# A graph kernel whose edges are sorted further ahead of their scatter, with x loaded after the scatters

## The chip, the cores and the metric

The kernel runs on one core of one Trainium2 chip. The metric is the device time of one execution in microseconds (us), the median of several runs. A core has five engines with an instruction stream each: PE multiplies matrices, DVE and ACT do elementwise work, POOL issues the scatters here, and SP issues most of the loads. Each engine runs its own instructions in order, and waits for the others by semaphores.

## The reference

6,250 nodes have 128 features each (x), and 206,250 edges have 128 features each. The edge features are summed onto the node that the edge starts from, and a small network is applied to each node. Cut to what matters:

```python
edge_aggr = jnp.zeros((n, HIDDEN)).at[src].add(edge_attr_128)
combined = jnp.concatenate([x, edge_aggr, global_expand], axis=-1) @ W_c + b_c
h = jax.nn.softplus(combined @ W1 + b1)
h = jax.nn.softplus(h @ W2 + b2)
return layernorm(x + (h @ W3 + b3))
```

The source nodes come in no useful order, and nothing is known of them before the launch, so the kernel has to sort the edges on the chip.

## The kernel before, in words

**Sorting.** The edges lie as 1,692 columns of 122 edges, and two columns are a *pair*: 846 pairs in 282 *pieces* of up to three pairs. Each pair goes through five steps. `load_rows` loads 8 pairs of edge rows from `in_edge` into a row buffer (`rows`, of which there are `ROWS` = 4), issued on SP. `code_rows` writes each row's code beside it (ACT, L1068). `compare` makes a one-hot matrix `sort_hot` from the positions of the edges (half on DVE at L1094, half on ACT at L1101 and L1103). `gather` multiplies it with the rows on PE (L1114), which puts the rows in the order of their buckets, into one of three PSUM banks. `settle` copies them on ACT (L1126) into one of `SETS` = 6 places, `pairs`. `scatter_row` then writes them with an indirect DMA from POOL (L1143) into `rows_by`, a table in DRAM with a stretch for every *bucket* of 196 nodes. A place is free again once its scatter has landed.

**Summing.** When a visit's scatters are done, `load(j)` reads up to eight chunks of 128 rows back from `rows_by` into one of six `chunks` buffers (SP). `match` compares their codes with the nodes (DVE, `hot`, L942), `product` multiplies on PE (`part`, L965), and `add` adds the result into `sums_t` (DVE, L988). A `part` matmul in the program is two instructions in the trace.

**The nodes.** After the last scatter come thirteen tiles of up to 512 nodes: `z_of(1, ...)` multiplies `x_t` (x turned, 128 x 6250) and `sums_t` with weights on PE (L1306 and L1307), two more layers follow (L1310, L1345), then x is added from `x_sb`, and the rows are normalised and stored. The sums of the last visits are done between these tiles. POOL adds the last bias to `x_sb` ahead of that.

**What sets the order.** On PE, DVE, ACT and SP the order of the instructions is written out by a plan, since each engine keeps to it. The plan gives each pair a scatter time, 1.3 us apart from 24 us on, and puts each step in at a fixed time ahead of that:

```python
SCATTER = 1.3
LOADED, CODED, COMPARED, GATHERED, SETTLED = 36.0, 21.0, 17.5, 14.0, 10.5
```

`when(t, step)` collects the steps, and they are sorted by time. The times only make the order; what an instruction waits for is set by its data. Chunk loads follow their last scatter's planned time by 11 us, matches and products come 9 and 10.5 us later. Every load on SP is issued by `sync_dma` (L283). `weights` loads the weights and x_t at planned time 100.

**Names that the text uses.** `first_at` is the planned scatter time of each load of rows, `begins` that of each piece. `pair_sets[i % SETS]` is the place of piece i. `node_rows_of` loads x for a tile of nodes (L293, its issue at L296). `ahead` is the pool that holds what the node tiles need, and `STRIDE` the number of chunks of 128 rows from one bucket's stretch in `rows_by` to the next bucket's.

Of the kernel before, what the change touches and what calls it, by code (L numbers as in the profile page):

```python
# [7 lines left out]
F32 = mybir.dt.float32  # L8
# [10 lines left out]
P = 128  # L19
# [32 lines left out]

FILL, DUE = 3, 8
ROW = 136
SETS = 6
FILL_BUCKETS = 4
FILLS, SLACK = 30.0, 60.0
HALF = 4
# [1 line left out]

SCATTER = 1.3
LOADED, CODED, COMPARED, GATHERED, SETTLED = 36.0, 21.0, 17.5, 14.0, 10.5
FIRST = 24.0
SOON, FLAGGED = 4.0, 15.9
SHARE = 2
# [9 lines left out]

SUMS = 2

ROWS = 4
BANKS = 3

TABLES = 6
# [61 lines left out]
def kernel(  # L143
# [115 lines left out]
    w_sb = {n: of_weights[n] for n in ("w1", "w2", "w3")}  # L259
    cols = of_weights["cols"]  # L260

    x_t = const.tile([P, N], F32, name="x_t")
    fold = const.tile([P, 2, D], F32, name="fold")
    z_bias = const.tile([P, 1], F32, name="z_bias")
    neg_z = const.tile([P, 1], F32, name="neg_z")
# [23 lines left out]
    def in_blocks(of, n0, lo, hi, r):  # L289
        at = next(k for k, (a, _) in enumerate(blocks) if a == n0 + lo * P) - lo  # L290
        return of[:r, at + lo:at + hi, :]

    def node_rows_of(pool, n0, n, bufs, load=sync_dma):  # L293
        t = pool.tile([P, 4, D], F32, name="x_sb", bufs=bufs)
        for lo, hi, r in blocks_of(n):
            load(t[:r, lo:hi, :], in_blocks(x, n0, lo, hi, r))  # L296
        return t

    sums_p = ctx.enter_context(tc.tile_pool(name="chunks", bufs=AHEAD))
    hots = ctx.enter_context(tc.tile_pool(name="hots", bufs=6))  # L300
# [8 lines left out]
    with ExitStack() as phase:  # L309
# [556 lines left out]
        def sum_steps():  # L866
# [36 lines left out]
            def load(j):  # L903
                v, col, _, all_of = loads[j]
                t = sums_p.tile([P, LOAD_CHUNKS, ROW], F32, name="chunks")
                chunks[j] = t
                assert len(scattered) >= col // 2
                at, q = [], 0
                while q < len(all_of):
                    of, b, c = all_of[q]  # L910
                    n = sum((o > 0) == (of > 0) and (of > 0 or x == b) for o, x, _ in all_of)
                    at.append((q, n, first_chunk(b + 1, True) + 2 * c if of else first_chunk(b) + c))
                    q += n
                for a, n, r in at:
                    ins = sync_dma(t[:, a:a + n].rearrange("p j c -> p (j c)"),
                                   rows_by[r * P:(r + n) * P, :].rearrange("(p j) c -> p (j c)", p=P))
                    late = scattered[max(0, col // 2 - LANES):col // 2] if col // 2 > awaits[0] else []
                    awaits[0] = max(awaits[0], col // 2)
                    for one in late:
                        tc.add_manual_dep(ins, one.name, SYNC, reason="every row is there")  # L920
                    apart(ins, "direct", ["scatter"], late)
# [233 lines left out]
        with tc.manual_schedule(engines={ET.PE, ET.DVE, ET.Activation, ET.SP}):  # L1155
# [31 lines left out]
            for i, (_, _, k) in enumerate(pieces):  # L1187
# [3 lines left out]
                    now += SCATTER  # L1191
                ends.append(now)
            first_at = [t for t, i, j in at_time][::LOAD_COLS // 2]
            early = [i for i, t in enumerate(first_at) if t < LOADED]
            last_pair = len(pieces) - 1
            load_rows(early[0])
# [3 lines left out]

            def weights():
                sync_dma(weights_sb, weights_in)
                for a in range(0, N, TURNED):
                    b = min(N, a + TURNED)
                    sync_dma(x_t[:, a:b], x_turned[:, a:b])

            assert G > 6
            events = []
# [5 lines left out]
                for k, step in enumerate(steps):  # L1214
                    when(t0 + (k + 0.5) / len(steps) * (t1 - t0), step)

            for i, t in enumerate(first_at):
                if t >= LOADED:
                    when(t - LOADED, lambda i=i: load_rows(i))
                when(t - CODED, lambda i=i: code_rows(i))  # L1220
            for i, t in enumerate(begins):
                mine = units(i)
                for u, unit in enumerate(mine):
                    late_by = SCATTER * pieces[i][2] * u / len(mine)
                    soon = 0.0 if i or u else SOON
                    when(t - COMPARED + late_by - soon, lambda unit=unit: compare(unit))
                    when(t - GATHERED + late_by - 1.7 * soon, lambda unit=unit: gather(unit))
                    when(t - SETTLED + late_by, lambda unit=unit: settle(unit))
# [67 lines left out]
    def node_layers(sums, ready):  # L1296
# [6 lines left out]
        def z_of(layer, n0, w):  # L1303
            z = bank()
            if layer == 1:
                nc.tensor.matmul(z[:, :w], fold[:, 0, :], x_t[:, n0:n0 + w], start=True, stop=False)  # L1306
                nc.tensor.matmul(z[:, :w], fold[:, 1, :], sums_t[:, n0:n0 + w],  # L1307
                                 start=False, stop=True)
            else:
                nc.tensor.matmul(z[:, :w], w_sb["w2"], h1.pop(n0)[:, :w], start=True, stop=True)  # L1310
            sub_z[layer, n0] = [z]
# [82 lines left out]
        with tc.manual_schedule(engines={ET.PE, ET.DVE, ET.Activation, ET.SP}):  # L1394
            part_of = {t: k for k, part in enumerate(parts) for t in part}
            now, steps = None, list(sums)

            def summed_to(k, most=None):
                while steps and ready() < sum(tiles[k]) and most != 0:
                    steps.pop(0)()  # L1400
                    most = most and most - 1

            for n0, w in tiles:
                x_of[n0] = node_rows_of(ahead, n0, w, len(tiles), load=nc.scalar.dma_start)
                for lo, hi, r in blocks_of(w):
                    nc.gpsimd.tensor_tensor(
                        x_of[n0][:r, lo:hi, :], x_of[n0][:r, lo:hi, :],
                        b3_all[:r].unsqueeze(1).to_broadcast([r, hi - lo, D]), op=ALU.add)
            summed_to(0)
            z_of(1, *tiles[0])  # L1410
            normed = None
            for step in range(len(tiles) + 2):
                first, second, third = (tiles[k] if 0 <= k < len(tiles) else None
                                        for k in (step, step - 1, step - 2))
                if step + 1 < len(tiles):
                    summed_to(step + 1, FIRST_STEPS)
                if second:
                    z_of(2, *second)
                if third:
                    k = part_of[third]  # L1420
                    if third == parts[k][0]:
                        now = open_part(parts[k])
                    last_product(*third)
                for layer, tile_ in ((1, first), (2, second)):
                    if tile_:
                        decay(layer, *tile_)
                        log1p(layer, *tile_)
                if third:
                    last_layer(now, *third)
                    if third == parts[k][-1]:  # L1430
                        normed = (now, k >= len(parts) - 2, k == len(parts) - 1)
                if step + 1 < len(tiles):
                    summed_to(step + 1)
                    z_of(1, *tiles[step + 1])
                for layer, tile_ in ((1, first), (2, second)):
                    if tile_:
                        softplus(layer, *tile_)
                if normed:
                    norm(*normed)
                    normed = None  # L1440
# [123 lines left out]
```

## Time and profile before

| | |
|---|---|
| median of 3 runs | 1329.86 us (1329.32 to 1330.11) |
| profiled execution, its own time | 1331.48 us |
| its span in the trace | 1329.7 us |
| mean granted TensorE clock | 0.953 |
| scatters (L1143) | 846, 978 ns each |
| moved by DMA | 386.29 MB, mean 291 GB/s |
| chunk loads issued on SP | 735 |

The profile is of one execution. A busy time is the sum of an engine's instructions; the rest of the span is idle time, which costs only where the engine is the one that the others wait for. A chain of waits is followed back from the last instruction: at each step to what released it.

### The profile page before, as it was taken

Reading aid. Unit: us, or ns where it says so; the run is one execution under the profiler, and the core shown is the slowest. Engines: PE = TensorE matmul, PEld = TensorE weight load, DVE = VectorE, ACT = ScalarE, POOL = GpSimd, SP = SyncE. Lnnn points to the kernel's source line nnn. Section 1 sums busy time; section 2 is a strip of 40 time slices with the busy share of each in tenths; the row PEclk is TensorE's granted clock in tenths of the full one; section 3 lists DMA queues with packets and bytes.
Section 4 is the critical chain, followed back from the end, with each engine's and each line's share of the span. In section 5 each row is a group of like instructions: output and inputs, shape, how many; then the busy total and the mean of one; then the engine's idle time right before and its main releaser. Section 6 shows DMA issues by size and latency. Waiting matters only on the chain.

```text
span 1329.7 us, 27151 instructions
## 1 busy us (share of the span) xinstructions
PE 1190.0 (89%) x8677; PEld 1127.4 (85%) x8677; DVE 1080.9 (81%) x2418; ACT 1067.6 (80%) x2484; POOL 880.4 (66%) x915
## 2 busy tenths in 40 slices
PE   5886888878999889988899999999989999999893
PEld 4776887877999889988799999989989999998762
DVE  7867988998899979798788887889857657787774
ACT  5896999899987899876999989979889999403354
POOL 2776777777776677765777777767767777820334
PEclk9768999989999899998999999999989999999996
DMA  8899999999999999999999999999999999975421
GB/s 215 255 278 352 317 314 306 314 281 353 337 310 306 342 348 351 334 322 281 327 281 298 327 311 327 324 296 327 330 317 294 314 336 318 341 213 148 137 86 52
DMA packets 226901, 386.29 MB, mean 291 GB/s; under 512 B 29660, under 2 KB 138916, under 8 KB 226368
## 3 DMA queue, kind: packets, MB, share of 16 engines
q1 hardware_dynamic: 183009, 264.95, 66.2%
q0 software_dynamic: 41328, 115.65, 24.8%
q10 hardware_dynamic: 2415, 3.87, 0.9%
q8 instruction: 73, 1.20, 0.4%
q14 instruction: 76, 0.62, 0.1%
HBM read 239.37 MB, written 149.57 MB: 292 GB/s over the span
## 4 chain that ended last, share of the span: by engine, by line
PE 41%; DMA 28%; DVE 16%; ACT 7%; issue 5%; POOL 3%; SPq 1%; ACTq 0%; DVEq 0%; POOLq 0%
PE part L965 24%; DMA chunks<-rows_by 12%; PE sorted L1114 12%; DMA rows<-in_edge 10%; DMA rows_by<-pairs,pair 5%; ACT pairs L1126 4%; DVE hot L942 3%; POOL rows_by L1143 3%; ACT sort_hot L1101 2%; DVE sort_hot L1094 1%; DVE pair_ib L486 1%; DVE past L715 1%; DVE sums_t L988 1%; PE small L545 1%; PE small L547 1%
## 5 line engine op out<-in xcount | busy, mean ns | idle before, releaser
L1143 POOL DMA_INDIRECT rows_by<-pairs,pair x846 | 827.8, 978 | 326.2 <-issue 202.3
L965 PE MATMUL part<-hot,chunks 128*128 128x196 f32 x3576 | 683.5, 335 | 9.9 <-DVE sums_t L988 7.0
L1126 ACT COPY pairs<-sorted 64x387 f32<-64x387 f32 (+2 forms) x1144 | 544.2, 476 | 81.9 <-PE sorted L1114 62.5
L965 PEld LDWEIGHTS part<-hot,chunks 128*128 128x128 f32 x3576 | 591.2, 192 | 18.9 <-DVE sums_t L988 8.4
L1114 PE MATMUL sorted<-rows,sort_hot 122*128 122x129 f32 x3384 | 506.7, 290 | 52.5 <-ACT pairs L1126 43.4
L1114 PEld LDWEIGHTS sorted<-rows,sort_hot 122*128 122x128 f32 x3384 | 461.1, 200 | 65.2 <-ACT pairs L1126 62.6
L942 DVE TENSOR_TENSOR hot<-chunks,both_ps 128x784 f32<-128x784 f32 (+3 forms) x558 | 436.3, 803 | 20.6 <-DMA chunks<-rows_by 20.2
L1101 ACT ACTIVATE sort_hot<-plain,slot 122x128 f32<-122x128 f32 x846 | 279.0, 393 | 11.4 <-DMA rows<-in_edge 5.5
L988 DVE TENSOR_TENSOR sums_t<-sums_t,part 128x392 f32<-128x392 f32 (+1 forms) x262 | 144.0, 549 | 130.6 <-PE part L965 129.2
L1103 ACT ACTIVATE sort_hot<-sort_hot,ones 122x384 f32<-122x384 f32 (+2 forms) x286 | 175.1, 612 | 9.3
L1094 DVE TENSOR_TENSOR sort_hot<-slot,both_ps 122x384 f32<-122x384 f32 (+2 forms) x286 | 155.0, 543 | 3.8 <-PE sorted L1114 3.2
L486 DVE TENSOR_TENSOR pair_ib<-pair_block,both_ps 122x512 bf16<-122x512 bf16 (+2 forms) x157 | 103.9, 667 | 0.3
L1387 POOL TENSOR_SCALAR y<-y,mv,rs 128x128 f32<-128x128 f32 x40 | 31.3, 789 | 108.2 <-issue 79.0
L564 DVE TENSOR_REDUCE slot<-small 122x16 f32<-122x512 f32 (+2 forms) x109 | 73.1, 671 | 15.0 <-PE small L547 14.8
L1317 ACT ACTIVATE away<-sorted,z_bias 128x512 f32<-128x512 f32 (+2 forms) x13 | 8.5, 656 | 77.7 <-PE sorted L1307 77.7
L545 PE MATMUL small<-pair_ib,half 122*122 122x512 bf16 (+2 forms) x109 | 44.2, 405 | 15.8 <-DVE slot L564 15.6
L1068 ACT COPY rows<-pair_i 122x16 f32<-122x16 f32 x106 | 22.7, 215 | 30.5 <-DMA rows<-in_edge 29.5
L547 PEld LDWEIGHTS <-starts_h 128*122 128x122 bf16 x236 | 26.0, 152 | 17.8 <-issue 13.5
L715 DVE TENSOR_TENSOR past<-both_ps,starts 128x512 f16<-128x512 f32 (+1 forms) x61 | 40.1, 668 | 0.8 <-PE small L730 0.6
L730 PEld LDWEIGHTS <-past 128*128 128x128 f16 x424 | 25.5, 100 | 17.0 <-DVE past L715 11.8
L730 PE MATMUL small<-jump,past 128*128 128x56 f16 (+3 forms) x424 | 29.4, 191 | 10.7 <-DVE past L715 7.8
L715 DVE TENSOR_TENSOR past<-both_ps,starts_late 128x512 f16<-128x512 f32 (+2 forms) x49 | 32.5, 665 | 0.0
(162 smaller groups left out, 522.5 us busy)
## 6 DMA issues: line engine op xcount, KB each, us to landing
rows<-in_edge SPq DMA_DIRECT2D x105, 903.0 KB
chunks<-rows_by SPq DMA_DIRECT2D x431, 136.0 KB
chunks<-rows_by SPq DMA_DIRECT2D x229, 204.0 KB
rows_by<-fill SPq DMA_DIRECT2D x21, 816.0 KB
chunks<-rows_by SPq DMA_DIRECT2D x52, 272.0 KB
rows_by<-pairs,pair POOLq DMA_INDIRECT x846
rows<-in_edge SPq DMA_DIRECT2D x105, 80.6 KB
rows_by<-fill SPq DMA_DIRECT2D x14, 544.0 KB
```

The costliest lines, as they stand in the source:

```text
L486: nc.vector.tensor_tensor(ib, pair_block[:, cols].unsqueeze(2).to_broadcast([PN, n, SB]), iota_ps[:PN, :SB].unsqueeze(1).to_broadcast([PN, ...
L564: nc.vector.tensor_reduce(to, of, axis=mybir.AxisListType.X, op=ALU.max)
L715: nc.vector.tensor_tensor(past[:, :, a:b], twice_ps[:KB].unsqueeze(1).unsqueeze(1).to_broadcast([KB, 2, b - a, P // 2]), own["starts"][:, ...
L942: nc.vector.tensor_tensor(hot[:, q - a:q - a + m], chunks[j][:, lo:hi + 1:step, D:W].to_broadcast([P, m, BL]), iota_ps.unsqueeze(1).to_bro ...
L965: nc.tensor.matmul(part[:, b - base_of[v], :], t[:, place_in(j, q), :D], hot[:, q - a], start=first, stop=last)
L988: nc.vector.tensor_add(here, here, of)
L1094: nc.vector.tensor_tensor(hot[:PN, :m], slot[:PN, at:at + 2 * m - 1:2].unsqueeze(2).to_broadcast([PN, m, P]), slot_ps[:PN].unsqueeze(1).to ...
L1101: nc.scalar.activation(hot[:PN, j], by_slot[:PN], AF.Abs, bias=slot[:PN, at:at + 1], scale=-1.0)
L1103: nc.scalar.activation(hot[:PN, :m], hot[:PN, :m], AF.Relu, bias=ones[:PN, :1], scale=-1.0)
L1114: nc.tensor.matmul(out[:, j, :], hot[:PN, j], rows_at[col // LOAD_COLS][:PN, col % LOAD_COLS, :], start=True, stop=True)
L1126: nc.scalar.copy(sets_at[i][64 * n:64 * n + 64, lo:lo + m, h, :W], out[64 * h:64 * h + 64, :m, :])
L1143: s = nc.gpsimd.indirect_dma_start(out=dst, out_offset=bass.IndirectOffsetOnAxis(ap=at, axis=0), in_=rows[:, j].rearrange("p a b -> p (a b ...
```

## The change

It does four things.

1. A function `earlier(t)` is taken off the planned times of `load_rows`, `code_rows`, `compare`, `gather` and `settle`. It is 0 up to a planned time of 44 us, grows by a tenth of the time from there, and stays at 14 us, or eleven pairs, from 184 us on. Scatters, chunk loads, matches and products keep their planned times.
2. There are eleven places for settled rows and five row buffers. Room comes from `x_t`, which held 25,000 bytes of each partition from the start and is now allocated in `ahead`.
3. x_t is no longer loaded by `weights` on SP. After the last settle, ACT issues x_t (three transfers of 1,024 KB and one of 53 KB) and all of x in one tile `x_rows` (three of 1,024 KB and one of 64 KB), in the place of 15 transfers into `x_sb`. POOL's addition of the bias follows on slices of `x_rows`.
4. Two chunk loads of the same shape whose rows lie `STRIDE` apart, those of two neighbouring buckets, are issued as one transfer with one more dimension.

```diff
-SETS = 6
+SETS = 11
+EARLIER, EASE, EASED = 14.0, 0.1, 20.0
-ROWS = 4
+ROWS = 5
...
-    x_t = const.tile([P, N], F32, name="x_t")
...
-                for a, n, r in at:
-                    ins = sync_dma(t[:, a:a + n].rearrange("p j c -> p (j c)"),
-                                   rows_by[r * P:(r + n) * P, :].rearrange("(p j) c -> p (j c)", p=P))
+                while at:
+                    a, n, r = at.pop(0)
+                    if at and at[0][1:] == (n, r + STRIDE):
+                        at.pop(0)
+                        b, r = divmod(r, STRIDE)
+                        ins = sync_dma(
+                            t[:, a:a + 2 * n].rearrange("p (h j) c -> p h (j c)", h=2),
+                            rows_by.rearrange("(s r) c -> s r c", r=STRIDE * P)[
+                                b:b + 2, r * P:(r + n) * P, :].rearrange("s (p j) c -> p s (j c)", p=P))
+                    else:
+                        ins = sync_dma(t[:, a:a + n].rearrange("p j c -> p (j c)"),
+                                       rows_by[r * P:(r + n) * P, :].rearrange("(p j) c -> p (j c)", p=P))
...
+            def earlier(t):
+                return max(0.0, min(EARLIER, EASE * (t - FIRST - EASED)))
...
             def weights():
                 sync_dma(weights_sb, weights_in)
-                for a in range(0, N, TURNED):
-                    b = min(N, a + TURNED)
-                    sync_dma(x_t[:, a:b], x_turned[:, a:b])
...
-            for i, t in enumerate(first_at):
-                if t >= LOADED:
+            for i, at in enumerate(first_at):
+                t = at - earlier(at)
+                if at >= LOADED:
                     when(t - LOADED, lambda i=i: load_rows(i))
                 when(t - CODED, lambda i=i: code_rows(i))
-            for i, t in enumerate(begins):
+            for i, at in enumerate(begins):
+                t = at - earlier(at)
                 mine = units(i)
...
+            x_t = ahead.tile([P, N], F32, name="x_t")
+            x_rows = ahead.tile([P, len(blocks), D], F32, name="x_rows")
+            for a in range(0, N, TURNED):
+                b = min(N, a + TURNED)
+                nc.scalar.dma_start(x_t[:, a:b], x_turned[:, a:b])
+            for a in range(0, len(blocks), TURNED // P):
+                b = min(len(blocks), a + TURNED // P)
+                nc.scalar.dma_start(x_rows[:, a:b, :], x[:, a:b, :])
+            x_of["t"] = x_t
...
-                x_of[n0] = node_rows_of(ahead, n0, w, len(tiles), load=nc.scalar.dma_start)
+                k = by_block.index(n0)
+                x_of[n0] = x_rows[:, k:k + -(-w // P), :]
```

Three places show how the order moves. The first is SP's queue around the load of the weights. Here `rows<-in_edge` is a load of edge rows (two instructions for one), `chunks<-rows_by` a chunk load, and `rows_by<-fill` clears rows of the table. Before:

```order
L283 DMA chunks<-rows_by 128x136 x12
L283 DMA rows_by<-fill 128x4x408
L283 DMA weights_sb<-in_weights 128x900
L283 DMA x_t<-in_x_turned 128x2048 x3
L283 DMA x_t<-in_x_turned 128x106
L283 DMA rows<-in_edge 112x4x516
L283 DMA rows<-in_edge 10x4x516
L283 DMA chunks<-rows_by 128x136 x4
```

After:

```order
L283 DMA chunks<-rows_by 128x2x136 x6
L283 DMA rows<-in_edge 112x4x516
L283 DMA rows<-in_edge 10x4x516
L283 DMA rows_by<-fill 128x4x408
L283 DMA weights_sb<-in_weights 128x900
L283 DMA rows<-in_edge 112x4x516
L283 DMA rows<-in_edge 10x4x516
L283 DMA chunks<-rows_by 128x2x136 x2
```

The four pieces of x_t are gone, a load of rows stands ahead of the weights that stood behind them, and twelve and four chunk loads are six and two of twice the size. In the whole program SP's chunk loads go from 735 to 689.

The second is PE's queue at the end of the sorting. `sorted<-rows,sort_hot` is a gather (L1114 before, L1117 after), `part<-hot,chunks` a product of the sums (L965 before, L968 after), and `small<-most_of,ones` a count at the end. Before:

```order
L1114 MATMUL sorted<-rows,sort_hot 128x129 x3
L965 MATMUL part<-hot,chunks 128x196 x4
L1114 MATMUL sorted<-rows,sort_hot 128x129 x4
L965 MATMUL part<-hot,chunks 128x196 x24
L1241 MATMUL small<-most_of,ones 1x48
L965 MATMUL part<-hot,chunks 128x196 x128
L1306 MATMUL sorted<-x_t,fold 128x512
```

After:

```order
L1117 MATMUL sorted<-rows,sort_hot 128x129 x3
L968 MATMUL part<-hot,chunks 128x196 x4
L1117 MATMUL sorted<-rows,sort_hot 128x129 x4
L968 MATMUL part<-hot,chunks 128x196 x49
L1247 MATMUL small<-most_of,ones 1x48
L968 MATMUL part<-hot,chunks 128x196 x128
L1312 MATMUL sorted<-x_t,fold 128x512
```

Behind the last gather stand 49 products where 24 stood, ahead of the same count; from there on the order is the same.

The third is ACT's queue at its last settles (`pairs<-sorted`, with the number of the place) and the loads of x. Before:

```order
L1126 COPY pairs_111<-sorted 64x2x129 x4
L296 DMA x_sb<-in_x 128x512 x11
L296 DMA x_sb<-in_x 128x128
L296 DMA x_sb<-in_x 120x128
L296 DMA x_sb<-in_x 128x256
L296 DMA x_sb<-in_x 114x128
```

After:

```order
L1129 COPY pairs_117<-sorted 64x2x129 x4
L1413 DMA x_t<-in_x_turned 128x2048 x3
L1413 DMA x_t<-in_x_turned 128x106
L1416 DMA x_rows<-in_x 128x2048 x3
L1416 DMA x_rows<-in_x 128x128
```

x_t now comes from this queue, ahead of x itself, in 8 issues for the 15 before, with 6.4 MB for 3.2.

More of the change, by code (lines that the diff above doesn't have):

```diff
@@ L291, in in_blocks @@
         return of[:r, at + lo:at + hi, :]
[L293 to L297, printed above, removed]
     sums_p = ctx.enter_context(tc.tile_pool(name="chunks", bufs=AHEAD))
@@ L1305, in z_of @@
             if layer == 1:
-                nc.tensor.matmul(z[:, :w], fold[:, 0, :], x_t[:, n0:n0 + w], start=True, stop=False)
+                nc.tensor.matmul(z[:, :w], fold[:, 0, :], x_of["t"][:, n0:n0 + w], start=True, stop=False)
                 nc.tensor.matmul(z[:, :w], fold[:, 1, :], sums_t[:, n0:n0 + w],
@@ L1401, in summed_to @@
                     most = most and most - 1
+            x_t = ahead.tile([P, N], F32, name="x_t")
[7 more added lines that the diff above has]
+            x_of["t"] = x_t
+            by_block = [n0 for n0, _ in blocks]
             for n0, w in tiles:
-                x_of[n0] = node_rows_of(ahead, n0, w, len(tiles), load=nc.scalar.dma_start)
+                k = by_block.index(n0)
+                x_of[n0] = x_rows[:, k:k + -(-w // P), :]
                 for lo, hi, r in blocks_of(w):
```

## The prediction

> **What bounds the kernel now.** I read the page's busy shares first, then the busy time by stretches, the chain of waits, the waits of each engine, and last the issues on SP and ACT around the places that the diff touches. The profiled execution took 1331.48 us, 1.62 us above the median of the three timed runs (1329.86); its span is 1329.7 us, so 1.8 us lie outside the span, and I leave them as they are.
>
> From the page, the busy time of the engine that works longest:
>
> ```profile
> PE 1190.0 (89%) x8677; PEld 1127.4 (85%) x8677; DVE 1080.9 (81%) x2418; ACT 1067.6 (80%) x2484; POOL 880.4 (66%) x915
> ```
>
> PE has 1329.7 - 1190.0 = 139.7 us in which it does no matmul. Nothing in the diff takes matmuls away, so a gain has to come out of these 139.7 us (or out of a better clock). The busy time by stretches says where they lie; the first column is the stretch and its length, then PE, PEld, DVE, ACT, POOL, the granted clock, the busy share of the DMA engines and GB/s:
>
> ```profile
> 50.00:650.00 600.00, 522.09 (x4125) 494.93 (x4126) 523.80 (x1273) 522.96 (x1234) 429.60 (x439) 0.93 0.99 318
> 650.00:1150.00 500.00, 486.83 (x3525) 478.63 (x3524) 382.80 (x687) 456.57 (x1076) 374.23 (x384) 0.98 1.02 315
> 1150.00:1330.00 180.00, 149.84 (x788) 127.29 (x786) 135.63 (x311) 55.30 (x95) 55.94 (x69) 0.94 0.47 144
> ```
>
> Three stages with three limits. Before 650 us PE is idle for 600 - 522.09 = 77.9 us; there the DMA engines are busy 0.99 of the time, and DVE and ACT are as busy as PE. From 650 to 1150 us PE is idle for 13.2 us in 500: this stage is PE's. After 1150 us it is idle for 30.2 us. So what saves time in the first stage lets PE arrive earlier at its full stretch, and what only lets the scatters run ahead of PE late in the kernel saves nothing. The waits say the same for POOL, which issues the scatters (engine and line, what it waited for, us in total, times, longest):
>
> ```profile
> POOL rows_by L1143 <- issue: 202.3, 661, 1.2
> DVE sums_t L988 <- PE part L965: 129.2, 112, 8.2
> POOL rows_by L1143 <- ACT pairs L1126: 56.4, 44, 7.2
> PE sorted L1114 <- ACT pairs L1126: 43.4, 39, 2.5
> ```
>
> 661 of the 846 scatters wait for nothing but their own issue, and 56.4 us is all that POOL ever waited for sorted rows to be settled. That is the most that settling them earlier can give POOL, and only a part of it reaches the end, since 112 times DVE waited for PE's sums.
>
> **The change part by part.**
>
> *x_t leaves the early SP queue.* The SP queue around its load, then the chain of waits there and later, each with start and length, and the POOL wait that followed:
>
> ```profile
> 101.38 3.88 SPq L283 DMA_DIRECT2D x_t<-in_x_turned  x4
> 105.38 1.64 SPq L283 DMA_DIRECT2D rows<-in_edge  x2
> 108.49 6.73 SPq L283 DMA_DIRECT2D chunks<-rows_by  x4
> ```
>
> ```profile
> 108.88 16.11 DMA chunks<-rows_by
> 125.08 0.56 DVE hot L942
> ...
> 132.55 6.72 DMA rows<-in_edge
> ...
> 140.17 4.18 DMA chunks<-rows_by
> ...
> 542.98 13.53 DMA rows<-in_edge
> 556.52 11.29 DMA chunks<-rows_by
> ...
> 588.08 15.07 DMA chunks<-rows_by
> ```
>
> ```profile
> 134.29 0.97 POOL L1143 DMA_INDIRECT rows_by<-pairs,pair  x1 [7.00 <-ACT pairs L1126]
> ```
>
> The four pieces of x_t (3.2 MB) stand ahead of a rows load and of the chunk loads, and the first chunk load behind them takes 16.11 us, on the chain; thirty us later one takes 4.18. POOL then stands for 7.00 us, its longest wait for settled rows. I price the stall by PE's idle time:
>
> ```profile
> 100.00:150.00 50.00, 34.84 (x306) 31.04 (x302) 41.92 (x119) 39.31 (x93) 32.96 (x35) 0.90 1.02 340
> 150.00:300.00 150.00, 128.61 (x1073) 121.11 (x1074) 134.99 (x327) 139.06 (x328) 114.37 (x118) 0.97 0.96 305
> ```
>
> In the 50 us of the load PE is idle for 15.16 us, and in the next 150 us for 21.39, or 7.13 in 50. The load costs 15.16 - 7.13 = **8.0 us**, which go. The ends: 3.9 us, if only SP's own issue time goes, and 16.11 - 4.18 = 11.9 us.
>
> *Sorting up to 14 us earlier, eleven places, a fifth row buffer.* Loads, codes, comparisons, gathers and settles move ahead together, so the distances between them stay; what grows is the lead over the scatter. It eases in from 44 us on, and what is pulled ahead of the chunk work then is work that PE does anyway. The price shows at PE's end: 49 part matmuls stand behind the last sort where 24 stood. Each is two instructions in the trace. The chain of waits there:
>
> ```profile
> 1144.32 0.99 PE sorted L1114 x8
> 1145.31 7.96 PE part L965 x48
> 1153.27 0.17 PE small L1241 x2
> 1153.45 10.49 PE part L965 x62
> ...
> 1164.29 3.13 DMA chunks<-rows_by
> ...
> 1171.28 27.13 PE part L965 x162
> 1198.41 0.86 PE sorted L1306 x2
> ```
>
> One instruction takes 7.96 / 48 = 0.166 us, so 25 x 2 x 0.166 = 8.3 us of work moves behind the last sort. It is not new work: PE reaches the last sort that much earlier if it was busy up to there, and the 30.2 us that PE idles at the end have room for it. I take 0, with +8.3 as the end at which those 8.3 us are not got back. What the lead can take away is a stall that feeds itself: a late chunk holds DVE, PE and with them the next sort, the scatters come late, and so do the chunks that wait for them. Settled rows in hand for 11 pairs more let POOL go on. Between 300 and 650 us,
>
> ```profile
> 300.00:650.00 350.00, 317.90 (x2466) 306.19 (x2466) 308.67 (x722) 299.28 (x706) 245.54 (x251) 0.96 1.01 328
> ```
>
> PE idles for 32.1 us; that and 0 are the ends. But the DMA engines are busy 1.01 of the time there, so a lead cannot make the bytes come faster. The one excess that a row buffer and a lead cover plainly is the rows load of 13.53 us at 543 us, against the 6.72 us of the one at 132.55: **6.8 us**, which I take; the chunk loads of 11.29 and 15.07 us behind it wait for scatters and stay. The fifth buffer also eases SP, by its own waits:
>
> ```profile
> SPq L283 <- PE part L965: 228.2, 118, 8.4
> SPq L283 <- PE sorted L1114: 158.0, 41, 16.6
> ```
>
> The 158.0 us are waits for a row buffer that PE still reads, and chunk loads and fills are queued behind them. I count them inside the 6.8, because SP also waits for 228.2 us on PE's parts and so would stand later.
>
> *Two alike chunk loads in one.* SP's chunk issues fall from 735 to 689. At 6.73 / 4 to 0.39 us each, the 46 that go are 18 us or more of SP's time, but SP stands 386 us in the two waits above. I take 0, with -2 and +1 as ends, the latter for a tile whose first half must now wait for its second. Bytes and packets stay.
>
> *x_t and x behind the scatters.* ACT now issues 8 transfers with 6.4 MB after its last settle, where it issued 15 with 3.2 MB:
>
> ```profile
> 1146.76 15.91 ACTq L296 DMA_DIRECT2D x_sb<-in_x  x12
> ```
>
> ACT has nothing else to do then. The stage in which they land:
>
> ```profile
> 1150.00:1200.00 50.00, 48.22 (x283) 46.34 (x282) 44.34 (x69) 0.00 (x0) 19.44 (x20) 1.00 0.80 246
> ```
>
> At 246 GB/s for a share of 0.80, a full share is 307 GB/s, so the added 3.2 MB are 10.4 us of DMA time, and 0.20 x 50 = 10 us were free. PE does not touch x_t before 1198.41, fifty us after the issue. The cover for the chunk loads is their six buffers: 8 chunks of two instructions each are 2.7 us a buffer, 13 us for five. A chunk load of 3.13 us stands on the chain already, so I take **+1**; the ends are 0 and +10.4, if the transfers push the chunk loads back by all that they take.
>
> Here a rule speaks against the change. The Trainium skill, DMA: Bandwidth & Descriptors, section Issuing engines are not separate DMA queues, says that transfers from all issuing engines run on the same 16 DMA engines, and that another issuer saves only the time it takes to issue. The row above with 3.88 us on SP is that issue time; by the rule x_t would save 3.9 us early and give back 10.4 late, +6.5 instead of -7. That the early stall of 16.11 us stands on the chain and the tail has a free fifth is why I do not take it.
>
> **The sum.** -8.0 - 6.8 + 0 + 0 + 1.0 = -13.8 us. 1331.48 - 13.8 = 1317.7 for an execution like the profiled one, and 1.62 less against the median: **1316 us**. The forecast's own range has x_t at its two ends and the lead between 0 and half of the 32.1 us: -3.9 + 0 + 1 = -2.9 gives 1327, -11.9 - 16 + 1 = -26.9 gives 1303.
>
> **The rivals.**
>
> *The stall breaks altogether (faster).* If the lead and the buffers remove all 32.1 us from 300 to 650 us as well as the 8.0 before, the sum is -40.1 and the time 1290 us. For it: the chain from 543 to 603 us is DMA and scatters, link after link, which is what a self-feeding stall looks like. Against it: the DMA share of 1.01.
>
> *The bytes are only moved (slower).* The mechanism is the queue of transfers at 1146 us: 6.4 MB from ACT beside the last chunk loads. It decides once a chunk load lands more than 13 us after it was free to go, the cover above. Then PE, at its full stretch there (48.22 of 50 us), starves for up to the 10.4 us, the 25 parts behind the last sort are work on the path (+8.3), and from the early stage only 3.9 us come back: +14.8 in all, 1344.7 us, or 1336.4 without the parts. I set it at 1341. For it: one chunk load on the chain in this stage already, and a DMA share of about 1 in all stages ahead, so that a stall removed early may simply return. Against: the free fifth. The Trainium skill's rule on issuing engines leads here.
>
> *Nothing changes.* If the DMA engines set the pace from 50 to 1150 us (0.99 and 1.02), the sorting lead is refilled at the same rate, and x_t's DMA time comes back in the tail: the time stays at 1330, give or take 2.7 us. Against it: GB/s differ between stretches of like share (305 to 340), so the share is no hard limit.
>
> **How the numbers follow.** Forecast 0.50, stall broken altogether 0.15, nothing changes 0.08, slower 0.27. A measurement of this kernel tells 0.2%, some 2.7 us, from no change. The forecast and the first rival are faster: 0.65; the same 0.08; slower 0.27. The range takes the forecast, most of the way to the first rival, and the slower rival up to its 1341: 1297 to 1341. It leaves out about 0.10 below and 0.09 above.
>
> **What would show it.** Right: no chunk load near 16 us on the chain around 109 us, POOL's 7.00 us wait gone, PE's idle time from 100 to 150 us near 7 us, and the last sort on PE about 20 us earlier than 1144 us (13.8 of gain, 8.3 of parts). POOL's waits for settled rows well under 56.4 us, without the end moving by as much. The first L1306 follows the parts without waiting for x_t. Wrong: PE busy under 45 us in the 50 us behind the last sort, with chunk loads of over 13 us on the chain there; or the last sort where it was, with the DMA share still at 1; or SP's wait for PE's sorts still near 158 us.

## The result: slower by 0.7%, and the profile after

| | before | after |
|---|---|---|
| median of 7 runs each | 1330.2 us (1329.32 to 1331.99) | 1341.06 us (1338.01 to 1347.99) |
| ratio, 95% interval | | 1.0073 (1.0046 to 1.0101) |
| profiled execution, its span | 1331.48, 1329.7 us | 1343.9, 1342.1 us |

The forecast was 1316 us. The time is that of the rival named slower, 1341, but not by its mechanism alone; that the number agrees is in part luck.

The page of the kernel after, and its busy time by stretches (columns as in the prediction):

```profile
PE 1194.4 (89%) x8677; PEld 1131.4 (84%) x8677; DVE 1080.6 (81%) x2418; ACT 1065.2 (79%) x2489; POOL 877.3 (65%) x915
```

```profile
50.00:650.00 600.00, 519.49 (x4087) 492.48 (x4086) 515.84 (x1256) 525.19 (x1244) 431.45 (x443) 0.93 0.97 312
650.00:1150.00 500.00, 486.53 (x3517) 478.56 (x3516) 383.28 (x691) 451.37 (x1066) 371.36 (x382) 0.98 1.01 311
1150.00:1342.00 192.00, 157.82 (x831) 134.25 (x829) 141.87 (x319) 55.19 (x95) 53.73 (x66) 0.94 0.50 161
```

PE's idle time in the first two stages has not moved: 80.5 us for 77.9 and 13.5 for 13.2. The last stage is longer, with more work in it and more idle time (34.2 us for 30.2). The chain of waits of the kernel after says where:

```profile
1143.22 0.89 PE sorted L1117 x8
1144.11 3.00 PE part L968 x18
1147.13 11.30 DMA chunks<-rows_by
...
1159.35 8.99 DMA chunks<-rows_by
...
1168.36 7.34 DMA chunks<-rows_by
...
1178.25 4.15 DMA chunks<-rows_by
...
1184.06 27.13 PE part L968 x162
1211.19 0.86 PE sorted L1312 x2
```

Before, the last sort ended at 1145.31 us and the first node tile began at 1198.41: 53.1 us. After, they are at 1144.11 and 1211.19: 67.1 us. From there to the end of the span it is 131.3 us before and 130.9 after. So the 12.4 us between the two spans are made in the stretch between the last sort and the first node tile: it is 14.0 us longer, while the last sort ends 1.2 us earlier and the end is 0.4 shorter. By the medians the kernel is only 10.9 us slower. With the same stretch and end, the last sort of a typical execution then comes some 2.7 us earlier (14.0 - 0.4 - 10.9, an estimate); the forecast had said about 20. Of the 14.0, 50 instructions of 0.166 us are 8.3: the 25 products that moved. The other 5.7 are waits, and four chunk loads of 4 to 11 us stand on the chain where one of 3.13 stood.

The early load of x_t did go. The first row is the wait that POOL had at 134.29 us, the second the stretch from 100 to 150 us:

```profile
133.73 0.97 POOL L1146 DMA_INDIRECT rows_by<-pairs,pair  x1 [0.30 <-issue]
```

```profile
100.00:150.00 50.00, 37.13 (x338) 33.21 (x337) 42.99 (x120) 45.45 (x109) 38.10 (x40) 0.97 0.87 284
```

POOL goes on after its own 0.30 us there. But PE is idle for 12.87 us in this stretch, not for 7. The products that the order had here stand later: PE works on products for 8.59 us in it, and for 13.47 in the run *x alone* below, which has x_t late and no lead. Long chunk loads are not gone either: the chain followed back from 140 us has one of 14.60 us, from 121.61 on.

The waits of the kernel after:

```profile
PE sorted L1117 <- ACT pairs L1129: 59.2, 55, 2.7
...
POOL rows_by L1146 <- ACT pairs L1129: 55.5, 49, 7.0
```

POOL waited for settled rows for 55.5 us where it waited for 56.4. A lead of eleven pairs in the plan has not become a lead on the chip. It can be measured pair by pair, from the end of the last settle of a pair's piece to the start of its scatter: on the mean of the 846 pairs this is 2.67 us before and 2.44 after (2.81 in a second profile of the kernel after), and never more than 7.1. PE's wait for ACT's settles has grown from 43.4 to 59.2 us. ACT's instructions near the end of the sorting, and POOL's scatters of the first piece in them, suggest why (start, length, what, how many in a row):

```profile
1127.96 1.97 ACT L1129 COPY pairs<-sorted 64x387 f32<-64x387 f32 x4
1129.95 0.99 ACT L1104 ACTIVATE sort_hot<-plain,slot 122x128 f32<-122x128 f32 x3
1130.97 0.62 ACT L1106 ACTIVATE sort_hot<-sort_hot,ones 122x384 f32<-122x384 f32 x1
1131.49 0.20 ACT L1071 COPY rows<-pair_i 122x12 f32<-122x12 f32 x1
1131.70 1.96 ACT L1129 COPY pairs<-sorted 64x387 f32<-64x387 f32 x4
1133.68 0.99 ACT L1104 ACTIVATE sort_hot<-plain,slot 122x128 f32<-122x128 f32 x3
1134.70 0.62 ACT L1106 ACTIVATE sort_hot<-sort_hot,ones 122x384 f32<-122x384 f32 x1
1135.33 1.96 ACT L1129 COPY pairs<-sorted 64x387 f32<-64x387 f32 x4
```

```profile
1130.85 0.97 POOL L1146 DMA_INDIRECT rows_by<-pairs,pair  x1 [0.30 <-issue]
1132.12 0.97 POOL L1146 DMA_INDIRECT rows_by<-pairs,pair  x1 [0.30 <-issue]
```

The first piece is settled at 1129.93, and its first scatter starts 0.92 us later. Nothing is free on ACT in these rows: a piece of three pairs takes it 1135.33 - 1131.70 = 3.63 us, and 3.74 where it also writes codes. POOL's cadence of 0.97 + 0.30 us makes 3.81 for the same three scatters. ACT gains 0.07 to 0.18 us a piece on POOL, so by this estimate a lead of 14 us takes 78 to 200 pieces without a stall (the trace has 286 pieces, of four settles each), and a single stall can take it away. ACT is not alone in this. From 650 to 1150 us it is busy for 451.37 of 500 us and PE for 486.53, and in the chain of the kernel before PE takes 1.33 + 0.67 us for half a piece and its share of products, 4.0 for a piece.

SP's waits:

```profile
SPq L283 <- PE part L968: 290.6, 130, 8.5
...
SPq L283 <- PE sorted L1117: 78.3, 32, 13.8
SPq L283 <- DVE hot L945: 55.5, 11, 13.8
```

SP's waits for PE's sorts fell by 79.7 us, which is the fifth buffer's doing (with four they are 175.4 in the run *after, four row buffers*). Its waits for PE's parts grew by 62.4 us, and those for DVE's `hot` by 35.9 (19.6 before).

### The profile page after: what moved, and what is told of

Read it like the earlier page. It is cut to its first block, busy times and chain, and to the rows that moved or that the text cites. A ratio compares the mean times of both kernels' runs of the same rounds, so it can differ in the third digit from the quotient of the medians.

```text
span 1342.1 us, 27057 instructions
## 1 busy us (share of the span) xinstructions
PE 1194.4 (89%) x8677; PEld 1131.4 (84%) x8677; DVE 1080.6 (81%) x2418; ACT 1065.2 (79%) x2489; POOL 877.3 (65%) x915
## 4 chain that ended last, share of the span: by engine, by line
PE 37%; DMA 24%; DVE 12%; POOL 9%; issue 8%; ACT 8%; SPq 1%; ACTq 0%; POOLq 0%; DVEq 0%
PE part L968 21%; PE sorted L1117 11%; DMA rows_by<-pairs,pair 10%; POOL rows_by L1146 9%; DMA chunks<-rows_by 9%; ACT pairs L1129 5%; DMA rows<-in_edge 3%; DVE hot L945 2%; ACT sort_hot L1104 2%; DMA rows_by<-fill 2%; DVE sort_hot L1097 1%; DVE slot L558 1%; PE small L539 1%; DVE past L709 1%; DVE pair_ib L480 1%
## 5 line engine op out<-in xcount | busy, mean ns | idle before, releaser
L968 PE MATMUL part<-hot,chunks 128*128 128x196 f32 x3576 | 689.6, 337 | 14.2 <-DVE sums_t L991 11.0
L968 PEld LDWEIGHTS part<-hot,chunks 128*128 128x128 f32 x3576 | 597.3, 194 | 23.5 <-DVE sums_t L991 13.0
L1117 PE MATMUL sorted<-rows,sort_hot 122*128 122x129 f32 x3384 | 506.7, 290 | 63.7 <-ACT pairs L1129 59.2
L1117 PEld LDWEIGHTS sorted<-rows,sort_hot 122*128 122x128 f32 x3384 | 460.7, 201 | 79.2 <-ACT pairs L1129 78.4
```

What stands on the lines that cost most here:

```text
L968: nc.tensor.matmul(part[:, b - base_of[v], :], t[:, place_in(j, q), :D], hot[:, q - a], start=first, stop=last)
L1117: nc.tensor.matmul(out[:, j, :], hot[:PN, j], rows_at[col // LOAD_COLS][:PN, col % LOAD_COLS, :], start=True, stop=True)
```

## The experiments

Two theories. *Late parts*: the lead never comes about, and the 25 products that it puts behind the last sort are work on the path. *x in the tail*: the 6.4 MB beside the last chunk loads are the loss. Single executions differ in when the last sort is done (1144.1 and 1138.6 us in two profiles of the kernel after, on two chips); the stretch from the last sort to the first node tile repeats to within a microsecond there (67.1 and 66.7 us), so it is read from the profiles and the times from the medians. Each ratio is to the kernel before on the same chip. In the table, the runs marked A were made on one chip and those marked B on another; for the first two rows the chip is not known.

| run | chip | products between last sort and first node tile | that stretch, us | ratio to before, 95% interval |
|---|---|---|---|---|
| before | | 152 | 53.1 | |
| after | | 177 | 67.1 | 1.0073 (1.0046 to 1.0101) |
| after, again | B | 177 | 66.7 | 1.0106 (1.0064 to 1.0148) |
| x alone | A | 152 | 56.5 | 1.0000 (0.9970 to 1.0030) |
| merged loads alone | A | 152 | 53.1 | 0.9998 (0.9968 to 1.0027) |
| x, fifth row buffer | B | 152 | 61.8 | 1.0037 (1.0008 to 1.0066) |
| after without the lead | A | 152 | 61.2 | 1.0036 (1.0010 to 1.0062) |
| the same, four row buffers | A | 152 | 57.1 | 0.9998 (0.9973 to 1.0024) |
| after, four row buffers | B | 177 | 65.0 | 1.0097 (1.0062 to 1.0131) |
| after, half the lead | A | 164 | 63.4 | 1.0060 (1.0034 to 1.0087) |
| after without x | A | 177 | 59.2 | 1.0048 (1.0020 to 1.0076) |
| after, x in three lots | A | 177 | 60.5 | 1.0086 (1.0053 to 1.0120) |

**x alone.** Places, row buffers, lead and chunk loads are as before; the edit is to the kernel after, with cuts marked.

```diff
-SETS = 11
+SETS = 6
...
-EARLIER, EASE, EASED = 14.0, 0.1, 20.0
+EARLIER, EASE, EASED = 0.0, 0.1, 20.0
...
-ROWS = 5
+ROWS = 4
...
-                    if at and at[0][1:] == (n, r + STRIDE):
+                    if False:
```

> The kernel before with x_t and x loaded from ACT after the last settle, and nothing else of the change. Theory (late parts): the loss is the 25 products behind the last sort, since the lead over the scatters never comes about; x alone then gains 8 us early and loses some 5 in the tail: 1325 to 1330 us. Rival (x in the tail): the 6.4 MB beside the last chunk loads are the loss and the early gain is given back by the shared transfers: 1337 to 1343 us, with several chunk loads of over 7 us on the chain behind the last sort.

1332.05 us beside 1333.88: no change. The chain behind its last sort:

```profile
1144.75 0.97 PE sorted L1117 x8
1145.72 7.96 PE part L968 x48
...
1159.77 8.62 DMA chunks<-rows_by
...
1171.54 9.13 DMA chunks<-rows_by
...
1182.41 4.73 DMA chunks<-rows_by
...
1202.23 0.86 PE sorted L1312 x2
```

Three chunk loads of 8.62, 9.13 and 4.73 us stand on it, and the stretch is 3.4 us longer than before. The early gain is there in its place:

```profile
100.00:150.00 50.00, 41.50 (x331) 37.57 (x332) 45.66 (x124) 44.19 (x105) 37.06 (x39) 0.90 0.96 306
```

PE is idle for 8.5 us in the stretch where it was idle for 15.16, and the 100th scatter starts at 153.2 us for 159.9 before. But in these two profiles the gain is used up on the way: the 500th scatter starts at 699.3 for 701.9, the 800th at 1094.7 for 1095.3, and the last sort ends at 1145.7 for 1145.3. Neither theory's number was met; the theory of x in the tail as all of the loss is out.

**After without the lead.** `EARLIER = 0.0`, all else as after.

> The changed kernel with the planned times of sorting as before (EARLIER = 0), all else kept: eleven places, five row buffers, x in the tail, merged chunk loads. Theory (late parts): 24 products behind the last sort instead of 49, 8 us or more less than the changed kernel: 1322 to 1331 us. Rival (x in the tail): 1337 to 1343 us, as the changed kernel.

1337.73 us, ratio 1.0036. The time lies just inside the rival's range, but the kernel before took 1333.88 us on that chip; by the ratio the loss is half of the first 1.0073. The intervals overlap. If both numbers hold, the lead is a part of the loss, and something in the places, the fifth buffer or the merged loads costs too.

**Lead alone**, on the kernel before, with six places and x_t loaded early.

```diff
+EARLIER, EASE, EASED = 14.0, 0.1, 20.0
...
+                t = at - earlier(at)
```

> The kernel before with only the planned times of sorting moved up to 14 us ahead; six places, four row buffers, x_t early, chunk loads apart. Theory (late parts): 49 products behind the last sort and no earlier sorts: +6 to +10 us, 1336 to 1341. Rival (x in the tail): no loss, 1326 to 1332 us.

2190.97 us. Six places hold 18 pairs, 23.4 us of the plan, and a settle now stands 24.5 us ahead of its scatter, so places are written over before they are scattered: what is summed changes, and ACT waits 206 times for scatters to land:

```profile
ACT pairs L1127 <- DMA rows_by<-pairs,pair: 905.1, 206, 9.8
```

It does not price the lead, but it shows that this lead cannot stand without the additional places.

**Merged loads alone.** The kernel before, with the fourth part of the change.

> The kernel before with only the chunk loads of two buckets merged. Both theories: SP's issue time is not on the path, 1328 to 1332 us. A third view, that a merged transfer lands later and holds up its first half, would give 1333 to 1340 us.

1332.37 beside 1333.88 us, 0.9998: nothing, as forecast.

**After without x.**

```diff
...
-                nc.scalar.dma_start(x_t[:, a:b], x_turned[:, a:b])
...
-                nc.scalar.dma_start(x_rows[:, a:b, :], x[:, a:b, :])
+            nc.gpsimd.memset(x_t, 0.0)
+            nc.gpsimd.memset(x_rows, 0.0)
```

> The changed kernel without the eight transfers of x_t and x: POOL fills both tiles with zeros instead, so x is left out of the result. Theory (two prices): of the changed kernel's 11 us, 8 are the products that stand behind the last sort and stay, and some 5 are chunk loads held up behind the last sort, which go: 1333 to 1338 us, chunk loads of 3 to 6 us there. Rival (x in the tail is all of the loss): 1322 to 1330 us.

1335.83 us, ratio 1.0048, inside the range of the two prices together. The chain behind its last sort:

```profile
1139.67 0.71 PE sorted L1117 x4
1140.38 16.25 PE part L968 x98
1156.63 0.18 PE small L1247 x2
1156.81 42.74 PE part L968 x256
1199.55 0.86 PE sorted L1312 x2
```

Without the transfers no chunk load is on the chain at all, and 354 product instructions run in one piece: 59.0 us of PE's own work for the 50.5 that 304 take. So the transfers of x cost 67.1 - 59.2 = 7.9 us of the stretch, and products alone set what is left. Its 6.1 us over the 53.1 before are less than the 8.3 of the moved products, since the waits that the kernel before has there are gone too.

**x in three lots.** The first 2 MB after the last settle, the next after the first tile's work on ACT, the rest after the fourth's.

> The changed kernel with x loaded in three lots: 2 MB after the last settle, 2 MB after the first tile's work on ACT, the rest after the fourth's. Theory (two prices): half to all of the 5 us of the tail come back, 1334 to 1338 us. Rival (x in the tail is all): 1324 to 1331 us. If the size of the transfers and not their number holds up the chunk loads, nothing comes back: 1339 to 1343.

The stretch falls to 60.5 us, 6.6 less than after; the stretch from the first node tile to the end is 134.5 - 130.9 = 3.6 us longer. The median, 1342.18 us, shows no gain within its interval. The expectation of 1334 to 1338 was missed: the time lies in the range given for nothing coming back, though the stretch itself did shrink.

**Half the lead.** `EARLIER = 7.0`.

> The changed kernel with a lead of 7 us instead of 14 (EARLIER), all else kept: 36 products behind the last sort instead of 49. Theory (late parts): 13 products less are 4.3 us: 1335 to 1339 us. Rival (the lead is no part of the loss): 1339 to 1343 us, as the changed kernel.

1339.31 us, ratio 1.0060, at the 1339 that parts the two ranges. Its interval overlaps that of the full lead, and that of no lead too, so the step does not tell a dose.

**Without the lead, four row buffers.** `EARLIER = 0.0`, `ROWS = 4`.

> As the run without the lead, but with four row buffers again. The run without the lead stood at 1.0036 of the kernel before and x alone at 1.000; between them lie the fifth buffer, the five more places and the merged loads. If the fifth buffer costs it, by letting rows loads in ahead of chunk loads: 1328 to 1333 us, with SP's waits for PE's sorts near 160 us. If the merged loads beside x cost it: 1335 to 1340 us.

1328.98 us, ratio 0.9998, like x alone. All of the change without lead and fifth buffer is neither faster nor slower.

**After again, and after with four row buffers** (`ROWS = 4`), side by side.

> The changed kernel once more, on the same chip as the three runs beside it: ratio 1.0046 to 1.0101 again, about 1336 to 1344 us.

> The changed kernel with four row buffers, lead and all else kept. Theory (fifth buffer): without a lead the fifth buffer alone made the difference between 1.0036 and 0.9998, so 5 us go here too: 1333 to 1337 us, with SP waiting some 160 us for PE's sorts again. Rival (the lead is the loss, the buffer is not): 1339 to 1343 us.

1340.8 and 1343.3 us. The fifth buffer costs nothing that shows once the lead is there; my expectation of 1333 to 1337 fell. The run above, without the lead and with four row buffers, differs from the second of these in the lead alone: 0.9998 without the lead, 1.0097 with it. The intervals lie apart (up to 1.0024, from 1.0062), so the lead is the loss, as far as ratios taken on two chips tell. In the stretch behind the last sort the two differ by 65.0 - 57.1 = 7.9 us, about the 8.3 us of the moved products. PE's wait for ACT's settles is 53.7 to 63.8 us in the five profiles with the full lead and eleven places on chips of this pace, and 39.5 to 50.2 in the six without one.

**x and the fifth buffer.** As x alone, with `ROWS = 5`.

> The kernel with x alone moved (ratio 1.000) plus a fifth row buffer: six places, no lead, no merged loads. Theory (fifth buffer): 1334 to 1339 us, ratio 1.002 to 1.006. Rival (it took the places or the merged loads too): 1328 to 1333 us.

1334.33 us, 1.0037: without a lead the fifth buffer seems to cost by itself, here as in the pair 1.0036 and 0.9998 above, though in each pair the intervals overlap a little. The stretch behind the last sort is 5.3 us longer with it (61.8 for 56.5 us).

**Double the lead.** `EARLIER = 28.0`.

> The changed kernel with a lead of 28 us (EARLIER), 72 products behind the last sort for 49. Theory (late parts): 23 products more are 7.6 us: 1346 to 1352 us. Rival (the lead's loss was paid once, for instance by the first tens of us, or there is none): 1338 to 1344 us. If more lead at last lets PE fill its idle time, less than the changed kernel.

1527.5 us, and no price of late products: where a piece has one pair, eleven places hold 31 pairs or 40.3 us of the plan, a settle stands 38.5 us ahead and comes ahead of the last scatter of its place, as in the run with the lead alone, and again other rows are summed.

The remaining six runs fell on chips on which the kernel before takes 1609 and 1634 us; of them only ratios and stretches are used, and their times are not put beside the others.

**The lead with the products moved along**, and with four row buffers. Chunk loads, matches and products are planned earlier too.

```diff
-PREP, LAG = 0.85, 11.0
+PREP, LAG = 0.85, 6.0
...
-MATCHED, MULTIPLIED, RATE = 9.0, 1.5, 0.58
+MATCHED, MULTIPLIED, RATE = 0.0, 1.5, 0.58
...
-ROWS = 5
+ROWS = 4
```

> The changed kernel with four row buffers and its lead of 14 us, but chunk loads 5 us and matches and products 14 us earlier in the plan too (LAG 6, MATCHED 0), so that PE's order has 152 products between the last sort and the first node tile, as before, and not 177. Theory (late parts): ratio 0.997 to 1.003, as without a lead. Rival (the sorting's own loads and places): 1.007 to 1.012, as with the lead.

Ratio 1.0001 (0.9977 to 1.0025): no loss, as the theory of late parts had it, with no run of the lead alone beside it on that chip. The stretch does not fit so well: with 152 products it is still 64.1 us, with chunk loads of 9.83, 7.55 and 6.83 us on the chain. The last sort ends at 1412.9 us, 8.3 earlier than in the run *no early x_t* below, which has the kernel before's order and was made on the same chip.

**Late products without a lead.** The kernel before with `MATCHED = 16.0`.

> The kernel before, with nothing of the change, but matches and products planned 7 us later (MATCHED 16): 181 products between the last sort and the first node tile for 152. Theory (late parts): 29 products of 0.33 us are 9.6 us, ratio 1.005 to 1.009. Rival: 0.998 to 1.002.

Ratio 1.0107 (1.0076 to 1.0138), which is 17 us, or 22 by the medians: more than the 9.6 us of the products. The chain behind its last sort:

```profile
1427.31 4.31 PE part L965 x26
...
1435.70 5.56 PE part L965 x16
...
1441.51 48.79 PE part L965 x292
1490.54 4.88 PE part L965 x28
1495.42 0.86 PE sorted L1306 x2
```

68.1 us, with no transfer of x on the chain and nothing of the change in the kernel. (362 instructions of 0.166 us are 60.1; 4.07 more, from 1431.63, are put down to another core or an unknown queue.) So products planned later do cost, without any lead. But this edit costs more than that: from the first node tile to the end it takes 139.5 us, for 131.2 in the run *no early x_t* on the same chip, and the change does not lengthen that part. Its 1.0107 is therefore no price of the 29 products alone.

**Early products.** The kernel before with `MATCHED = 4.0`.

> The kernel before with matches and products planned 5 us earlier (MATCHED 4): 144 products between the last sort and the first node tile for 152. Theory (late parts): 8 products less are 2.7 us, ratio 0.996 to 1.000, unless PE then waits for chunks: above 1.002. Rival: 1.000.

Ratio 0.9976 (0.9950 to 1.0001): the expected side, and the interval just takes in no change.

**No early x_t.** The kernel before with x_t filled with zeros instead of loaded.

> The kernel before without its early load of x_t, which POOL fills with zeros ahead of the first scatter; x itself is loaded as before, so the first layer lacks x. If the early load costs the 8 us of the forecast and they reach the end: 1321 to 1325 us, ratio 0.993 to 0.996. If they are given back on the way, by the DMA engines or DVE: 0.998 to 1.002.

Ratio 0.9999 (0.9974 to 1.0024). On that chip, where the DMA engines are busy 0.82 of the time from 50 to 800 us, the early load costs nothing that reaches the end, to within the interval. Whether it does where the kernel takes 1330 us was not run.

**The lead, with and without the products moved along, on one chip.**

> The lead with chunk loads, matches and products moved along (LAG 6, MATCHED 0), once more, beside the lead alone. Theory (late parts): ratio 0.997 to 1.003. Rival (the sorting's own loads and places): as the lead alone beside it, 1.007 or more.

> The lead alone (four row buffers), on the same chip as the run beside it. Theory (late parts): 1.006 to 1.013. Rival: the same as the run beside it.

Ratios 1.0013 (0.9985 to 1.0040) with, 1.0033 (1.0007 to 1.0059) without. They stand in the order expected, but the intervals overlap, and the lead alone missed the 1.006 to 1.013 of both theories: here it costs a third of what chip B showed. The stretch behind the last sort is 60.2 and 66.4 us.

## Why the prediction was wrong, point by point

**x_t's early load, -8.0: right in place, but it did not reach the end.** POOL's stall at 134 us is gone, and where x alone was moved PE's idle time from 100 to 150 us fell by 15.16 - 8.5 = 6.7 us. No gain is left in that run's time (1.0000) or where x_t was left out (0.9999). In its profile the 6.7 us shrink to 0.6 by the 800th scatter. What takes them back was not tested.

**The lead, -6.8: the step that failed.** I let "settled rows in hand for 11 pairs more" carry POOL over a late load. They were never in hand: from settle to scatter a pair has 2.44 us, where it had 2.67, and not 14 more. The wait of POOL for settled rows stayed at 55.5 us, and PE idles for 34.4 us from 300 to 650 us, where 32.1 were to become 25. The prediction moved the planned times and did not ask whether ACT and PE can run faster than POOL uses up. Where ACT runs without a gap it needs 3.63 to 3.74 us for the piece that POOL scatters in 3.81. The page's 80% for ACT is an average over stages; from 650 to 1150 us it is 90%.

**The 25 products, taken as 0: the other failure, and the larger.** I argued that PE would reach the last sort 8.3 us earlier, because it was busy up to there. It did not: PE's wait for settles grew by 15.8 us instead, and the last sort came 1.2 us earlier in the profile, some 2.7 by the medians. PE and ACT are both near full there; the reading that fits is that taking work from one only lets it wait for the other. So the end that I had priced, +8.3, is what happened: the stretch grows by 7.9 us between the runs that differ in the lead alone. The forecast's own range, 1303 to 1327, had left that end out, and the tail's +10.4 too; only the slower rival carried them. By their ratios (0.9998 and 1.0097) the same runs differ by about 13 us, on two chips; on another chip the lead alone cost 1.0033, about 5. That products in the wrong place are the mechanism is the likeliest reading; the test on one chip leaves it short of shown, and what lies over 8.3 us stays open.

**The tail, +1: too small.** With x alone the stretch grows by 3.4 us; in the kernel after the waits add 5.7, and leaving the transfers out gives 7.9 back. The free fifth of the DMA engines was an average over 50 us, and the transfers come at its start: the chunk load on the chain at 1147.13 took 11.30 us, inside the 13 us of cover that I counted. But the cover is only there if six buffers are full at that moment, and the chain shows that after 18 product instructions PE already waited. The rival's mechanism, the queue of transfers, was right in kind. Its claim that the bytes are only moved agrees with x alone, 1.0000. The Trainium skill, DMA: Bandwidth & Descriptors, section Issuing engines are not separate DMA queues, says that transfers run on the same 16 DMA engines whichever engine started them. Moving x_t from SP to ACT gained nothing at the end (1.0000), which agrees.

**Merged loads, 0: right.** 0.9998.

**The fifth buffer, inside the 6.8: no gain, and likely a cost.** SP's waits for PE's sorts halved, and SP "would stand later" was also right, but I did not ask what else the earlier issues collide with. Without a lead the two runs with the buffer are 0.4% slower than the kernel before, and the two without it are not. How is not settled.

## What to carry to other kernels

A place in the plan is not time in hand: before a lead is priced, compare the pace of the engine that must build it with that of the engine that uses it up, in the stage itself (3.63 us against 3.81 here). Work that an order puts behind the last producer is work at the end unless the engine really arrives earlier, and "busy" does not say that it will: two engines near full can wait for one another (PE 59.2 us for ACT's settles and ACT 59.0 us for PE's sorts here). A gain early on may be used up on the way (6.7 us here), so look for it again at the end. Price what is moved out of a crowded stretch at the first moments of the stretch it goes to, not at that stretch's mean.

## What was not expected of the hardware

The same program takes 1330 us on some chips and 1609 to 1634 on others, at a granted clock of 0.95 and about 0.90. Part of the page of a run on the second kind, the lead with the products moved along:

```profile
PE 1300.5 (81%) x8677; PEld 1201.4 (75%) x8677; DVE 1082.7 (67%) x2418; ACT 1064.1 (66%) x2489; POOL 876.7 (55%) x915
...
DMA packets 224613, 386.29 MB, mean 240 GB/s; under 512 B 28759, under 2 KB 137653, under 8 KB 223697
```

DVE, ACT and POOL are busy as long as ever; PE is busy longer (1300.5 us for 1194.4), and 240 GB/s are moved for 288. And the chunk loads on the chain beside transfers of a megabyte landed in 4 to 11 us, where the one on the chain before took 3.13. The size of the transfers is not shown to be the cause: with merged loads alone, beside transfers of 256 KB, one on the chain took 8.66 us.
